# Four graph layers in one program: waits counted by tile, the symmetry proof's buffers kept into the next layer's prologue, and small loads moved to another queue

## The chip, the cores and the metric

The kernel runs on one core of one Trainium2 chip. A core has a matrix engine (PE, its weight loads listed apart as PEld), a vector engine (DVE), a scalar engine (ACT), GpSimd (POOL) and SyncE (SP), which here only issues transfers. Each takes its own list of instructions in order and waits for the others by semaphores. Transfers between the chip's memory and the on-chip memory are carried by 16 DMA engines, whichever engine issued them. The metric is the device time in microseconds (us); lower is better.

## The reference

Four layers of a graph network on 4096 nodes with 128 features share one dense adjacency matrix of 4096 x 4096 numbers, all 0 or 1, symmetric, with ones on the diagonal. Each layer's result is added to its input and normalised by rows.

```
x = layernorm(x + L0(x, adj))   # hyperbolic: sigmoid attention over distances, adj * sigmoid(logits) times local log maps
x = layernorm(x + L1(x, adj))   # 4 heads: softmax of q k / sqrt(32) where adj is not 0; then a gate with x @ Ws
x = layernorm(x + L2(x, adj))   # relu( D^-1/2 (adj + I) D^-1/2 x W )
x = layernorm(x + L3(x, adj))   # leaky_relu(s_i + r_j) where adj > 0, softmax by rows, times x @ W.T + b
```

The kernel may not assume that the matrix is symmetric and holds only 0 and 1. It runs a fast form that needs both, checks them on the way, and at the very end starts the general form (class `Net`) if a check failed. In the runs here the fast form (class `Fast`) does all the work.

## The kernel before

**Tiling.** The matrix is cut into 8 x 8 blocks of 512 x 512 (`NS` = 8, `S` = 512), each held as 128 partitions x 4 x 512. The program writes two copies of the blocks into the chip's memory: `adjb` in bf16 (0.5 MB a block) and `adjf` in float32 (1 MB a block).

**Layer 0** (L315 to L612). A prologue computes the nodes' hyperbolic features `HT` and `HA`. `pair_loop` (L1716) then goes over the 36 block pairs with I <= J in an order written out by hand (`SHARED_ORDER`, inside `manual_schedule`, where each engine gets its instructions in the order of the source). Meanwhile GpSimd's queue writes `adjb` (`narrow`, L1919). After the loop an epilogue (L514 to L612) brings the sums into `X` and normalises them, in groups of four row tiles: products of H and X (L540), squares (L544), scalings (L535), and at the end `X` normalised by ScalarE (L235).

**The proof of symmetry** (`mirror`, L1671 to L1709) is written into the source right after the pair loop. For each pair of blocks it loads `low` (block I, J; L1690) and `up` (block J, I; L1693), three buffers each, and PE forms `low` minus the transposed `up` with scaled identities (`sized`, L1684), twelve 128-row pieces in one psum bank `pm` (two buffers), each piece with its own power of two. DVE then takes the largest absolute value (L1709). There are 28 pairs and 8 diagonal blocks. This part and the epilogue are not ordered by hand: a scheduler orders each engine's instructions, by their place in the source (their priority) and by what it takes to be ready.

**Layer 1** (`layer1`, L2164). Its prologue (L2200 to L2255) transposes `X` into `XT` (L166, 32 times on PE), makes q and k for 8 column chunks (`pqk`, L2215), splits each into two float32r parts (`cut`, L2217 and L2218, seven buffers) and stores them to memory (`qk`, L2224, 16 stores of 0.5 MB). `stack` (L2192) reads them back on GpSimd's queue in another layout, as `KS` and `QS`. Then come V (`VA`, L2230 and L2231), R (in `Y`, L2240 and L2241), and a bound on the logits (`pb`, `good`). `attention_unshifted` (L1948) is again ordered by hand: for 8 column blocks I and 32 row tiles jb it does scores (`ps`, L2007), exponentials (`e`, L2014, ACT), the mask (L2016, DVE), and, two steps behind, the sums (`pv`, L2033, PE). At every fourth step SP loads the next `at` block from `adjb` (L1966) and copies one block to `adjf` (L1969); ACT's queue loads rows of the matrix (`nat`, L1983), for degrees and for the check that all entries are 0 or 1. `ending(I)` (L2042 to L2116) turns sums into `X` and the scaled node rows `Y`.

**Layers 2 and 3** (`layers23`, L2259). A ring of 8 float32 blocks (64 KB of each partition) is filled by SP from `adjf` (`load`, L2337). Layer 2 splits `Y` into two float32r parts (`halve`, L2359 to L2363: the node parts `Y0` and `Y1`) and multiplies them with 64 ring blocks (`convolve`, L2382; the first products, L2374, go by `identr`, a copy of the identity). DVE looks at each block once more (`look`, L2346). Eight blocks more start layer 3 (`attend_first`, L2400), whose other 56 follow in `attend_factored` (L1535 to L1580).

**Pools and waits.** Buffers come from pools that open and close like a stack. When a pool lands on bytes of pools already closed, all its tiles wait for every user of those pools. A tile is a buffer of such a pool.

Of the kernel before, what the change touches and what calls it, by code (L numbers as in the profile page):

```python
# [9 lines left out]
F32 = mybir.dt.float32  # L10
# [51 lines left out]
class Net:  # L62
# [30 lines left out]

    def copies(self):
        self.adjT = self.dram.tile([self.NS, self.NS, P, 4, S], F32, tag="adjT", name="adjT")

    def pools(self, ctx, adj, big, t, o):

        self.on_scalar = 4
        if adj:  # L100
            self.adjp = ctx.enter_context(self.tc.tile_pool(name="adjp", bufs=adj))
        if big:
            self.ps_big = ctx.enter_context(self.tc.tile_pool(name="ps_big", bufs=big, space=PSUM))
        self.ps_t = ctx.enter_context(self.tc.tile_pool(name="ps_t", bufs=t, space=PSUM))
        self.ps_o = ctx.enter_context(self.tc.tile_pool(name="ps_o", bufs=o, space=PSUM))
# [26 lines left out]
    def load_row(self, vec, name, pool=None):  # L132

        t = (pool or self.const).tile([P, vec.shape[0]], F32, tag=name, name=name)
        self.nc.sync.dma_start(out=t, in_=vec.partition_broadcast(P))
        return t
# [7 lines left out]
    def load_mat(self, mat, name, pool=None):  # L144
        t = (pool or self.const).tile(list(mat.shape), F32, tag=name, name=name)
        self.nc.sync.dma_start(out=t, in_=mat)
        return t
# [163 lines left out]
    def layer0(self, x, weight, bias, att_w, att_b):  # L311
# [4 lines left out]
        with ExitStack() as ctx:  # L316
            self.on_scalar = 4
            keep = ctx.enter_context(tc.tile_pool(name="keep0", bufs=1))
            self.cols = ctx.enter_context(tc.tile_pool(name="cols0", bufs=1))
            adp = ctx.enter_context(tc.tile_pool(name="ad0", bufs=2))  # L320
            pre_pools = ctx.enter_context(ExitStack())
            pre = pre_pools.enter_context(tc.tile_pool(name="pre0", bufs=2))
            self.ps_t = pre_pools.enter_context(tc.tile_pool(name="ps_t", bufs=6, space=PSUM))
            one = pre_pools.enter_context(tc.tile_pool(name="one0", bufs=1))
            self.wide = pre_pools.enter_context(tc.tile_pool(name="wide", bufs=1))
            ps_c = pre_pools.enter_context(tc.tile_pool(name="ps_c", bufs=1, space=PSUM))
# [187 lines left out]
            late = ctx.enter_context(tc.tile_pool(name="late0", bufs=1))  # L514
            rot = ctx.enter_context(tc.tile_pool(name="rot0", bufs=6))
# [92 lines left out]
    def pair_loop(self, HT, HA, dr, rows, adp, early, rows4):  # L608
# [7 lines left out]
        with ExitStack() as ctx:  # L616
            atp = ctx.enter_context(tc.tile_pool(name="at0", bufs=2))
            wtp = ctx.enter_context(tc.tile_pool(name="sg0", bufs=6))
            wk = ctx.enter_context(tc.tile_pool(name="wk0", bufs=2))
            ps_t = ctx.enter_context(tc.tile_pool(name="ps_t0", bufs=2, space=PSUM))  # L620
            ps_z = ctx.enter_context(tc.tile_pool(name="ps_z0", bufs=2, space=PSUM))
            ps_i = ctx.enter_context(tc.tile_pool(name="ps_i0", bufs=1, space=PSUM))
            ps_j = ctx.enter_context(tc.tile_pool(name="ps_j0", bufs=1, space=PSUM))
# [224 lines left out]
    def layer1(self, Wq, bq, Wk, bk, Wv, bv, Ws, bs, Wb, R):  # L848
# [6 lines left out]
        with ExitStack() as ctx:  # L855
            self.on_scalar = 4
            keep = ctx.enter_context(tc.tile_pool(name="keep1", bufs=1))
# [27 lines left out]
            with ExitStack() as pctx:  # L885
                pre = pctx.enter_context(tc.tile_pool(name="pre1", bufs=1))
                rot = pctx.enter_context(tc.tile_pool(name="rot1", bufs=2))
                self.ps_t = pctx.enter_context(tc.tile_pool(name="ps_t", bufs=8, space=PSUM))
# [59 lines left out]
    def attention_unshifted(self, VA, KS, QS, at0, stack, R, wb):  # L948
# [4 lines left out]
        with ExitStack() as ctx:  # L953
            rot = ctx.enter_context(tc.tile_pool(name="rotf", bufs=1))
            natp = ctx.enter_context(tc.tile_pool(name="natf", bufs=2))
            atp = ctx.enter_context(tc.tile_pool(name="atf", bufs=1))
            ep = ctx.enter_context(tc.tile_pool(name="ef", bufs=3))
            ps_s = ctx.enter_context(tc.tile_pool(name="ps_s", bufs=3, space=PSUM))
            ps_v = ctx.enter_context(tc.tile_pool(name="ps_v", bufs=1, space=PSUM))
# [198 lines left out]
    def attention_shifted(self, V, qk, R, wb, spare):  # L1158
# [4 lines left out]
        with ExitStack() as ctx:  # L1163
            self.pools(ctx, 1, 2, 3, 1)
            self.wide = ctx.enter_context(tc.tile_pool(name="wide", bufs=2))
            keep = ctx.enter_context(tc.tile_pool(name="keeps", bufs=1))
            self.cols = ctx.enter_context(tc.tile_pool(name="cols1", bufs=1))
# [12 lines left out]
            work = ctx.enter_context(tc.tile_pool(name="work1", bufs=1))  # L1180
# [98 lines left out]
    def layers23(self, w2, weight, bias, a_s, a_r, out, Y):  # L1279
# [6 lines left out]
        with ExitStack() as ctx:  # L1286
            RING = 8
            ring = ctx.enter_context(tc.tile_pool(name="ring", bufs=1)).tile([P, RING, 4, S], F32, tag="ring", name="ring")
            keep = ctx.enter_context(tc.tile_pool(name="keep3", bufs=1))
# [10 lines left out]
            pre = pctx.enter_context(tc.tile_pool(name="pre3", bufs=1))  # L1300
            rot = pctx.enter_context(tc.tile_pool(name="rot2", bufs=2))
            wp = pctx.enter_context(tc.tile_pool(name="w2", bufs=4))
            ps_b = pctx.enter_context(tc.tile_pool(name="ps_b", bufs=2, space=PSUM))
            ps_t = pctx.enter_context(tc.tile_pool(name="ps_t", bufs=2, space=PSUM))
# [1282 lines left out]
```

## Time and profile before

| what | us |
|---|---|
| median of 3 runs (lowest, highest) | 2021.89 (2018.53, 2024.26) |
| the profiled execution, its own time | 2022.37 |
| its span, first to last instruction | 2020.6 |

| stage | about, us from the span's start |
|---|---|
| layer 0: prologue | 0 to 75 |
| layer 0: pair loop | 75 to 643 |
| layer 0: epilogue, beside the proof of symmetry | 643 to 717 (proof to 742) |
| layer 1: prologue | 742 to 786 |
| layer 1: attention | 786 to 1600 |
| layer 2 and the start of layer 3 | 1601 to 1801 |
| layer 3 | 1801 to 2020 |

A profile page gives busy times of each engine, then the span in 40 slices. A row of a group or of the timeline names line, engine, operation and "output<-inputs", sizes, and in brackets how long the engine idled before it and what ended that. PE's busy time is modelled and counts pipelined products. The page's slices:

```profile
PE   4789999999998677999999999999999798899997
...
DVE  6579999898898846789998999999999888888986
...
DMA  3488999898934978996767676768656699978882
```

Each digit is the busy share of a fiftieth of a millisecond (50.5 us) in tenths. PE is nearly full but for the first slices, for slices 13 to 15 (657 to 808 us), where layer 0 ends and layer 1 begins, and for slice 31 (1566 to 1616), between attention and layer 2.

### The profile page before, as it was taken

The page shows a single profiled execution, that of the slowest core. Times are in us where ns is not written, and L with a number is a line of the kernel's source. Part 1 is how long each engine was busy: PE and PEld are TensorE (multiplying, and loading weights), DVE is VectorE, ACT ScalarE, POOL GpSimd, SP SyncE. Part 2 cuts the span into 40 slices and gives each one's busy share as a digit, 9 for nine tenths or more (in the row PEclk, how much of TensorE's full clock was granted, in tenths as well). Part 3 has the DMA queues.
Part 4 walks back from the last instruction along what each step waited for, and adds up shares of the span by engine and source line. Part 5 has one row for each costly group of instructions (what it writes and reads, how often), then busy time and mean ns, then how long its engine had stood idle before and what let it go on. Part 6 is the DMA issues. An engine that isn't in the chain of part 4 may idle for free.

```text
span 2020.6 us, 23440 instructions
## 1 busy us (share of the span) xinstructions
PE 1861.8 (92%) x8406; PEld 997.6 (49%) x8420; DVE 1738.0 (86%) x2741; ACT 1319.2 (65%) x1665; POOL 171.7 (8%) x269
## 2 busy tenths in 40 slices
PE   4789999999998677999999999999999798899997
PEld 4257776667667455333333333333333476644443
DVE  6579999898898846789998999999999888888986
ACT  5589999999997733777878787777877422210000
POOL 2212111121100311200000000000000000000000
PEclk8569999899998997999999999999999899999999
DMA  3488999898934978996767676768656699978882
GB/s 102 49 141 142 156 151 169 144 177 147 156 111 168 373 263 284 259 267 217 236 215 236 211 230 208 239 215 240 211 209 240 238 422 420 421 281 321 295 278 84
DMA packets 167247, 450.86 MB, mean 223 GB/s; under 512 B 13708, under 2 KB 56876, under 8 KB 142544
## 3 DMA queue, kind: packets, MB, share of 16 engines
q1 hardware_dynamic: 112128, 330.94, 45.3%
q0 software_dynamic: 45632, 50.69, 19.8%
q10 hardware_dynamic: 9360, 67.64, 10.4%
q8 instruction: 68, 1.11, 0.2%
q14 instruction: 59, 0.48, 0.1%
HBM read 472.20 MB, written 111.23 MB: 289 GB/s over the span
## 4 chain that ended last, share of the span: by engine, by line
PE 44%; DVE 25%; ACT 15%; DMA 11%; issue 5%; SPq 0%; ACTq 0%; POOL 0%; DVEq 0%; POOLq 0%
PE pv L2033 11%; PE pa L1576 10%; DVE e L2016 9%; PE ps L2007 6%; ACT e L2014 4%; DMA ring<-adjf 4%; PE pz L1782 4%; DMA up<-adjb 3%; PE pi L1866 2%; DVE nat L1998 2%; PE pj L1881 2%; ACT w L1799 2%; ACT s L1822 2%; PE pz L1785 2%; ACT y L1818 1%
## 5 line engine op out<-in xcount | busy, mean ns | idle before, releaser
L2016 DVE SCALAR_TENSOR_TENSOR e<-at,e 128x2048 f32<-128x2048 bf16 x256 | 582.7, 2286 | 78.4 <-ACT e L2014 77.8
L2014 ACT ACTIVATE e<-ps 128x1024 f32<-128x1024 f32 x512 | 493.1, 1024 | 150.0 <-PE ps L2007 122.0
L2033 PE MATMUL pv<-e,VA 128*64 128x512 f32 x2048 | 497.5, 607 | 6.4 <-DVE e L2016 6.1
L2007 PE MATMUL ps<-QS,KS 128*128 128x512 f32 x1024 | 314.4, 425 | 11.1 <-ACT e L2014 10.4
L2007 PEld LDWEIGHTS ps<-QS,KS 128*128 128x128 f32 x1024 | 170.5, 188 | 238.5 <-ACT e L2014 180.2
L2033 PEld LDWEIGHTS pv<-e,VA 128*64 128x64 f32 x2048 | 124.8, 136 | 250.2 <-issue 214.1
L1576 PE MATMUL pa<-w,Y 128*128 128x512 f32 x448 | 195.3, 594 | 0.0
L1782 PE MATMUL pz<-HT 128*128 128x512 f32 x288 | 173.5, 687 | 10.2 <-DVE w L1854 9.1
L1573 DVE SCALAR_TENSOR_TENSOR w<-rho,col,ring 128x512 f32<-128x512 f32 x224 | 162.8, 747 | 22.3 <-PE pa L1576 9.7
L1866 PE MATMUL pi<-HA,w 128*128 128x129 f32 x1152 | 157.5, 286 | 7.3 <-ACT s L1822 5.3
L1866 PEld LDWEIGHTS pi<-HA,w 128*128 128x128 f32 x1152 | 144.0, 199 | 19.1 <-issue 9.3
L2382 PE MATMUL pa<-ring,Y 128*128 128x512 f32 x512 | 133.1, 411 | 11.9 <-DVE ring L2357 10.0
L1576 PEld LDWEIGHTS pa<-w,Y 128*128 128x128 f32 x448 | 83.7, 190 | 106.1 <-issue 79.9
L1989 ACT ACTIVATE nat<-nat 128x2048 f32<-128x2048 f32 x64 | 122.5, 1915 | 4.1 <-DMA nat<-in_adj_dram 4.1
L1791 DVE TENSOR_SCALAR t<-pz 128x512 f32<-128x512 f32 x144 | 93.7, 684 | 30.3 <-PE pz L1785 30.3
L1881 PE MATMUL pj<-HA,w 128*128 128x129 f32 x896 | 117.5, 288 | 2.1 <-DVE X L1895 1.8
L2382 PEld LDWEIGHTS pa<-ring,Y 128*128 128x128 f32 x512 | 95.9, 192 | 42.3 <-DVE ring L2357 12.8
L1881 PEld LDWEIGHTS pj<-HA,w 128*128 128x128 f32 x896 | 109.9, 200 | 9.9 <-issue 7.2
L1854 DVE TENSOR_TENSOR w<-w,ptz 128x512 f32<-128x512 f32 x112 | 73.7, 681 | 23.5 <-PE ptz L1849 23.3
L1799 ACT ACTIVATE w<-di,dr 128x512 f32<-128x512 f32 x144 | 90.6, 708 | 1.9 <-DMA di<-rows 1.9
L2346 DVE SCALAR_TENSOR_TENSOR odd<-ring 128x1024 bf16<-128x1024 f32 x64 | 78.1, 1220 | 12.8 <-DMA ring<-adjf 12.3
L1830 DVE SCALAR_TENSOR_TENSOR t<-t,s 128x2048 f32<-128x2048 f32 x36 | 82.3, 2285 | 6.7 <-ACT s L1822 6.7
(410 smaller groups left out, 2338.5 us busy)
## 6 DMA issues: line engine op xcount, KB each, us to landing
ring<-adjf SPq DMA_DIRECT2D x128, 1024.0 KB, 12.9
nat<-in_adj_dram ACTq DMA_DIRECT2D x64, 1024.0 KB, 6.0
adjf<-in_adj_dram SPq DMA_DIRECT2D x64, 1024.0 KB, 7.4
ad<-in_adj_dram SPq DMA_DIRECT2D x36, 1024.0 KB, 9.2
adjb<-in_adj_dram POOLq DMA_DIRECT2D x64, 512.0 KB, 11.5
at<-adjb SPq DMA_DIRECT2D x63, 512.0 KB, 3.5
low<-adjb SPq DMA_DIRECT2D x36, 512.0 KB, 5.5
up<-adjb SPq DMA_DIRECT2D x28, 512.0 KB, 6.7
```

Of the source, the lines that this page charges most:

```text
L1573: nc.vector.scalar_tensor_tensor(w, rho[:, I * S : (I + 1) * S], col[:, 0, j : j + 1], at[:, jb, :], op0=ALU.max, op1=ALU.mult)
L1576: nc.tensor.matmul(pa, lhsT=F[:, j, :], rhs=w, start=False, stop=(j == NT - 1), skip_group_check=True)
L1782: nc.tensor.matmul(pz, lhsT=HT[:, j * P : (j + 1) * P], rhs=HT[:, I * S : (I + 1) * S], start=True, stop=False)
L1799: nc.scalar.activation(w[:, jb, :], st[p]["d"][k], AF.Sigmoid, bias=dr[:, 4 * J + jb : 4 * J + jb + 1])
L1866: nc.tensor.matmul(row[I, "po"][ib // 2][:, ib % 2, :], lhsT=st[p]["w0"][:, jb, ib * P : (ib + 1) * P], rhs=HA[:, 4 * J + jb, :], start=False,
L1881: nc.tensor.matmul(pj[:, a, :], lhsT=st[p]["w1"][:, ib, jb * P : (jb + 1) * P], rhs=HA[:, 4 * I + ib, :], start=(ib == 0), stop=(ib == 3),)
L1989: nc.scalar.activation(nat, nat, AF.Identity, accum_out=self.deg2[:, k, i : i + 1])
L2007: nc.tensor.matmul(p[:, h, :], lhsT=KS[:, h2 + h, jb * P : (jb + 1) * P], rhs=QS[I % 2][:, h2 + h, :], start=True, stop=True,)
L2014: nc.scalar.activation(e[:, h2 : h2 + 2, :], p, AF.Exp)
L2016: nc.vector.scalar_tensor_tensor(e, at[:, jb % 4, :].unsqueeze(1).to_broadcast([P, NH, S]), 0.0, e, op0=ALU.not_equal, op1=ALU.mult,)
L2033: nc.tensor.matmul(st["po"][h // 2][g : g + 64, :], lhsT=VA[:, o : o + 64], rhs=e[:, h, :], start=(jb == 0), stop=(jb == NT - 1), skip_gro ...
L2382: nc.tensor.matmul(st["pa"], lhsT=halves[k][:, j, :], rhs=at[:, jb, :], start=(I > 0 and j == k == 0), stop=(j == NT - 1 and k == 1), skip ...
```

## The change

Four things. (1) The pools of the fast form are opened with `reuse_waits="tile"`: a tile that lands on bytes of closed pools waits only for the users of earlier tiles on its own bytes (in psum, its own bank). (2) The proof's three pools no longer close with layer 0. They are opened on the other side of the on-chip memory (`side="right"`), kept in `self.proof`, and close with layer 1's prologue; the prologue is given a priority ahead of the proof's (`high_priority`, from `self.rank`, which is the proof's place). To make room, the prologue has six psum banks for eight and five `cut` buffers for seven. (3) The node parts `Y0` and `Y1` get a pool of their own directly behind the ring. (4) The small loads of layers 2 and 3 (`w2`, `br3`, `wn3` and the three columns `ac`) go by GpSimd's queue, not SP's.

```diff
+    waits = "pool"
+
+    def pool(self, **kw):
+        return self.tc.tile_pool(reuse_waits=self.waits, **kw)
+
...
-    def load_row(self, vec, name, pool=None):
+    def load_row(self, vec, name, pool=None, queue=None):
...
-        self.nc.sync.dma_start(out=t, in_=vec.partition_broadcast(P))
+        (queue or self.nc.sync).dma_start(out=t, in_=vec.partition_broadcast(P))
...
-    def load_mat(self, mat, name, pool=None):
+    def load_mat(self, mat, name, pool=None, queue=None):
...
-            keep = ctx.enter_context(tc.tile_pool(name="keep0", bufs=1))
+            keep = ctx.enter_context(self.pool(name="keep0", bufs=1))
...
 class Fast(Net):
 
     MARKS = 160
+    waits = "tile"
...
-        keep = ctx.enter_context(tc.tile_pool(name="mir", bufs=1))
-        rot = ctx.enter_context(tc.tile_pool(name="mirt", bufs=3))
-        ps = ctx.enter_context(tc.tile_pool(name="mirp", bufs=2, space=PSUM))
+        self.proof, self.rank = ExitStack(), tc.cur_priority
+        keep = self.proof.enter_context(self.pool(name="mir", bufs=1, side="right"))
+        rot = self.proof.enter_context(self.pool(name="mirt", bufs=3, side="right"))
+        ps = self.proof.enter_context(self.pool(name="mirp", bufs=2, space=PSUM, side="right"))
...
             with ExitStack() as pctx:
-                pre = pctx.enter_context(tc.tile_pool(name="pre1", bufs=1))
-                rot = pctx.enter_context(tc.tile_pool(name="rot1", bufs=2))
-                self.ps_t = pctx.enter_context(tc.tile_pool(name="ps_t", bufs=8, space=PSUM))
+                pctx.enter_context(self.proof)
+                pctx.enter_context(tc.high_priority(tc.cur_priority - self.rank + 1))
+                pre = pctx.enter_context(self.pool(name="pre1", bufs=1))
+                rot = pctx.enter_context(self.pool(name="rot1", bufs=2))
+                self.ps_t = pctx.enter_context(self.pool(name="ps_t", bufs=6, space=PSUM))
...
-                        cut = rot.tile([P, 2, S], F32R, tag="cut", name="cut", bufs=7)
+                        cut = rot.tile([P, 2, S], F32R, tag="cut", name="cut", bufs=5)
...
+            halved = ctx.enter_context(self.pool(name="halved", bufs=1))
+            halves = [halved.tile([P, NT, D], F32R, tag=f"Y{k}", name=f"Y{k}") for k in range(2)]
...
-            halves = [pre.tile([P, NT, D], F32R, tag=f"Y{k}", name=f"Y{k}") for k in range(2)]
...
-            w = self.load_mat(w2, "w2")
-            br = self.load_row(bias, "br3", keep)
-            wn = self.load_mat(weight, "wn3", pre)
+            w = self.load_mat(w2, "w2", queue=nc.gpsimd)
+            br = self.load_row(bias, "br3", keep, nc.gpsimd)
+            wn = self.load_mat(weight, "wn3", pre, nc.gpsimd)
...
-                nc.sync.dma_start(out=ac[:, k : k + 1], in_=v.unsqueeze(1))
+                nc.gpsimd.dma_start(out=ac[:, k : k + 1], in_=v.unsqueeze(1))
```

All other pools of the layers change from `tc.tile_pool(...)` to `self.pool(...)` in the same way as `keep0`; the pools of constants, of `X` and of the memory copies do not. No arithmetic is added or left out.

## The prediction

> **What bounds the kernel now.** I read the whole-page view first: TensorE (PE) is busy 92% of 2020.6 us, VectorE (DVE) 86%. An average hides where a change of waits can pay, so I went on to the slices of the page, which dip at two places, and asked the waits, the chain of waits and the timeline there. The first place is the end of layer 0 and the prologue of layer 1. The chain of waits (start, length, what):
>
> ```profile
> 728.21 4.99 DMA low<-adjb
> ...
> 742.50 3.69 PE pt L166 x32
> ...
> 773.48 14.82 DMA qk<-cut
> ...
> 795.91 3.61 PE pv L2033 x8
> ...
> 800.85 1.87 PE pv L2033 x8
> ```
>
> and what was waited for between 640 and 800 us (total, times, longest):
>
> ```profile
> POOL VA L2204 <- PE pm L1704: 54.3, 1, 54.3
> ...
> ACT XT L181 <- PE pt L166: 27.6, 1, 27.6
> ...
> ACT L2014 <- DMA qk<-cut: 16.4, 1, 16.4
> ```
>
> The proof of symmetry (L1690 to L1709) runs from 643 to 741.7 and only then layer 1's first transposition starts, at 742.50. Its input was ready long before; ScalarE's last normalising of X:
>
> ```profile
> 715.65 1.65 ACT L235 ACTIVATE X<-X,ms,rs 128x128 f32<-128x128 f32 x4 [0.44 <-DVE ms L229]
> ```
>
> So X waits 25.2 us (717.3 to 742.5) for the proof. The table of windows gives the DMA share (second number from the end) and GB/s (last):
>
> ```profile
> 716.00:720.00 4.00, 2.36 (x21) 1.25 (x20) 0.21 (x1) 1.29 (x4) 0.00 (x0) 1.00 1.01 379
> 724.00:728.00 4.00, 3.37 (x41) 2.43 (x40) 0.69 (x1) 0.00 (x0) 0.00 (x0) 1.00 0.68 212
> 744.00:748.00 4.00, 4.00 (x26) 2.98 (x24) 1.84 (x4) 2.80 (x6) 1.48 (x1) 1.00 0.11 43
> 764.00:768.00 4.00, 1.95 (x8) 1.65 (x8) 1.95 (x3) 1.38 (x2) 1.64 (x3) 0.72 1.14 382
> ```
>
> Proof and prologue are each limited by transfers, one after the other, and between them the DMA engines are half empty. The second place is the step from attention to layer 2 (timeline of the SP queue, of PE, and windows):
>
> ```profile
> 1587.58 1.97 SPq L2337 DMA_DIRECT2D ring<-adjf  x4
> 1600.41 0.33 SPq L135 DMA_DIRECT2D br<-in_L_gnn_b_dram  x1
> ...
> 1602.68 22.43 SPq L2337 DMA_DIRECT2D ring<-adjf  x13
> ```
>
> ```profile
> 1601.38 2.20 PE L2374 MATMUL pa<-identr,Y 128*128 128x128 f32 x8 [12.55 <-ACT Y L2362]
> ```
>
> ```profile
> 1590.00:1600.00 10.00, 0.00 (x0) 0.00 (x0) 8.66 (x45) 0.92 (x5) 0.00 (x0) 0.59 0.91 383
> 1600.00:1610.00 10.00, 8.61 (x34) 7.17 (x34) 7.71 (x18) 5.64 (x9) 0.00 (x0) 0.73 0.68 252
> 1610.00:1620.00 10.00, 10.00 (x49) 8.29 (x48) 9.05 (x22) 0.00 (x0) 0.00 (x0) 1.00 1.01 421
> ```
>
> PE idles 12.55 us, the fifth ring block is issued 13 us after the fourth, and from 1610 to 1780 the DMA share is 1.01: layer 2 is bound by its 1 MB blocks. Elsewhere there is nothing for waits to win: attention has PE busy 99% in the windows from 900 to 1400, layer 3 100% from 1800 to 1900. A shift made at either place therefore reaches the end.
>
> **What the Trainium skill says.** "PSUM — Partial Sum Buffer", section "Engine vs sequencer instructions": ScalarE, VectorE and GpSimd queues are strict FIFO, and matmuls start and complete in program order. The trace agrees (742.50 directly follows the proof's last matmul), so PE's order decides what can lie beside what. "DMA: Bandwidth & Descriptors", section "Issuing engines are not separate DMA queues": transfers from SP, ACT and GpSimd share the same 16 engines, and another queue saves issue time alone. The trace agrees: one queue or two, the share tops out near 1.0 to 1.15. No page bears on the rule by which a pool waits; I read that from the programs' instruction lists.
>
> **The change, part by part** (line numbers of before).
>
> *Proof beside the prologue.* The lists show what the scheduler made of it: PE does 361 of the proof's 678 matmuls, then mixes 125 more with the 32 transpositions, then pqk, V and R products with 50 between; 142 come after R, 90 of them in one lump just before the third step's scores and the first pv. SP issues 27 of 28 block pairs, all 16 qk stores, and then the last pair and the 8 diagonal blocks. DVE's first masking of e stands behind the proof's last reduction. So the prologue can start when X is ready, but the first pv still waits for the whole proof. That makes it a sum over the DMA engines.
> Start: the first three pairs no longer wait for the pair loop's last matmul, but for a DVE step near 627, so they are there when PE is free at 643. From 643 the engines must move: 58 blocks x 0.524 MB = 30.4 MB at 372 GB/s (mean of the windows 644 to 724) = 81.7 us; at0, 16 stores of 0.524 and 16 loads of 0.262 MB = 13.1 MB at 381 (windows 760 to 784) = 34.4; one at, one adjf and one nat block, 2.6 MB at 370 = 7.1. Together 123.2, to 766.2 if they never rest. X does not hold this up: PE reaches the 361st matmul (18 pairs) near 691 and waits for the first X to about 697 (701.4 in before, less about 4 for the part below), but three pairs are in flight meanwhile. After the stores there are rests: the last pair and the diagonal come through three buffers, and a low block takes 5.5 us from issue to landing. Three rests of 3 us: 9 us (bounds 0 and 24). The proof ends at 775; its reduction 0.7 and the first e (2.29) bring the first pv to 778 and the second to 781, since e of later steps follows at 2.2. Before, the second pv was at 800.85. Gain 20 (29 to 5). The ps and e work that lay between (two table loads, three rounds) now hides under the proof's last blocks.
> Fewer buffers: cut 7 to 5, psum 8 to 6. In before the 12th cut already waits for stores; with five outstanding the engines still have 2.6 MB queued, so nothing to 2 us, in the range.
>
> *Waits by tile at the end of the pair loop.* DVE idles 4.4 us before 642.9 and ACT 11.1; the 24 scalings (2.5 us, L1684) and 28 of 32 squares (L544) move into that. Worth about 4 us on X, but X is not what comes last (see the sum); only the start of the loads counts, included above. At the pair loop's start the first pz waits for the copy of rows ending near 75.0 instead of the e2 step at 75.5: 0 to 0.7, I take 0.3.
>
> *Attention to layer 2.* The ring lies on KS. Its first load waited for the last pv (1587.49); by the list it now waits for the last ps (1580.87), and the six small loads that stood in SP's queue behind the fourth block (their tiles waited for the ending, 1600.4) are on GpSimd, so eight blocks go at once. Before, 0.36 + 3.83 + 2.52 MB moved by 1610; at 420 GB/s that is 16.0 us, as if saturated from 1594.0. After: 1580.9 plus the 1.5 us that before took from issue to flow (1587.6 to about 1589.1) = 1582.4. Gain 11.6. It holds while the engines never starve: a slot comes free when DVE has looked and PE has multiplied. Node parts (halve) now wait on VA's and QS's last users, 1587.5, not on the ending; identr is ahead of the ending on DVE, and PE starts near 1589.6 instead of 1601.4. DVE then carries the ending (10.4 us busy) between looks: eight looks by about 1614, one per 3 us against 2.6 for a block, with eight blocks of slack; enough. Over the stage DVE has 155.5 + 10.4 us of work in 180, PE 164 in 179. I take 11 (7 to 12).
> The GpSimd loads: w2 falls between two squares at 10.6 to 19.1, where POOL idles; wn waits for the last pv, then 64 KB, about 2.2 us by the skill's page on DMA ("Anatomy of one DMA — SWDGE (gpsimd) path": 2.0 us plus bytes/436 GB/s, an estimate; the 4 KB el loads here take 3.2). That is 1591; the products that need it come after three groups of 2.08 us, about 1596. Hidden; without that cover 1 to 3 us, but nobody queues behind it on POOL.
>
> *Sum:* 20 + 11 + 0.3 = 31. The profiled execution took 2022.37 (span 2020.6 and 1.8 around it), the median of the runs 2021.89: the same to 0.03%. 2022.4 - 31 = 1991.
>
> **Rivals.** (1) *The tail of the proof eats the gain.* The last pair and diagonal, behind the stores, meet adjf and nat, and each three-buffer turn takes as long as in the diagonal phase of before or longer (8 blocks in 14.3 us there). The proof ends near 790, the second pv at 796: gain 5 + 11 = 16, 2006. For: 142 matmuls in PE order before the first pv. Against: 3 us per block is twice what before needed.
> (2) *Layer 2 is not DMA bound once moved.* DVE with ending, parts and looks starves the slots, gain 3 there: 1999. For: DVE waits for ring in all only 12.3 us. Against: share 1.01 for 170 us.
> (3) *Slower.* One mechanism: SP's order. The at blocks of attention stand between proof blocks, which wait for PE, whose scores and pv stand behind the proof; a stalled store thus holds proof, attention and nat together. It decides from a first pv later than about 813 (795.9 + 11.3 won elsewhere + 6), 35 us past my 778; with the first pv at 826, 30 us later than before, the time is 2022.4 + 30 - 11 = 2041. Against: the same bytes would have to move at three quarters of the measured rates.
> (4) *It doesn't do what it says:* excluded by the lists for order; whether waits fall is rivals 1 and 2.
>
> **How the numbers follow.** Forecast 0.62 (1983 to 2000), rival 1 0.20, rival 2 0.10, rival 3 0.08. The range takes 1981 (proof's rests at nought: 29 + 12) to 2007 (rival 1), leaving out rival 3 and some of each edge. About 0.3%, 6 us, is what a measurement here can tell from no change. Faster: all of forecast and rival 2, most of rival 1, 0.89; within 0.3%: the edge of rival 1 and of 3, 0.05; slower 0.06.
>
> **What would show it.** First pqk near 714 (746.0 before) and no wait of POOL's VA memset for pm; DMA share near 1 from 645 to 760 without the dip at 744; first pv between 772 and 784; ring loads eight in a row from the last ps on; PE's gap before L2374 under 2 us. Wrong if the first pv comes after 790, if ring loads stop for more than 5 us before 1620's counterpart, or if attention itself (first pv to end of the last, 791.6 us) changes by more than 5 us.

## The result, and the profile after

| | before | after |
|---|---|---|
| median of 8 runs each, us | 2024.21 (2016.38 to 2028.32) | 2007.49 (1999.29 to 2012.74) |
| the profiled execution | 2022.37, span 2020.6 | 1999.29, span 1997.4 |

Ratio 0.9916, 95% interval 0.9893 to 0.9939: about 17 us, where 31 were forecast. A second series (six runs against eleven) gave 1998.89 against 2022.33, ratio 0.9884 (0.9855 to 0.9914). The two agree within their intervals, so the gain is 12 to 29 us as timed, and some 20 us if both are taken together. The traced execution was the fastest of the first eight, so I read stages from it beside two more traces of the same kernel; the one of the second series (1999.15 us) lies at that series' median.

The page's slices of the changed kernel (each digit is the busy share, in tenths, of 49.9 us, a twentieth of a millisecond; slices are counted from 0):

```profile
PE   4669999999998687999999999999999898899997
...
DMA  3468989899945896996767676768666899968881
```

PE still dips in slices 13 to 15 (649 to 799 us); in slice 31 it has 8 tenths for 7. Waits between 640 and 800 us (total, times, longest):

```profile
PEld pt L171 <- ACT X L240: 12.1, 15, 7.6
...
ACT e L2021 <- PE pm L1711: 10.6, 1, 10.6
```

The two long waits of before (POOL's memset of VA, and XT, both for the proof) have gone. Two new ones name the price: PE waits for X at a transposition, and the exponentials wait for the proof's products. The chain of waits:

```profile
692.39 0.86 PE pt L171 x2
...
713.75 0.88 PE pqk L2224 x2
...
768.74 7.24 DMA low<-adjb
...
782.13 2.29 DVE e L2023
784.55 1.94 PE pv L2040 x8
...
787.62 1.87 PE pv L2040 x8
```

The prologue's first product for q and k (`pqk`) starts at 713.75 instead of 746.0, yet the first pv only at 784.55 instead of 795.85, and the load just ahead on the chain is one of the proof's. The table of windows (the third number from the end is the clock, then DMA share and GB/s) shows where the transfers rest:

```profile
680.00:690.00 10.00, 3.86 (x40) 2.49 (x40) 8.02 (x32) 4.57 (x7) 3.65 (x1) 0.87 0.96 368
690.00:697.00 7.00, 4.61 (x25) 3.16 (x26) 6.35 (x36) 3.31 (x10) 0.00 (x0) 0.50 0.02 8
...
776.00:784.00 8.00, 7.13 (x50) 4.98 (x51) 2.48 (x2) 2.48 (x3) 0.00 (x0) 0.79 0.07 27
```

PE's timeline and SP's tell why:

```profile
684.75 0.38 PE L1706 MATMUL pm<-low,sized 128*128 128x512 bf16 x1
692.39 0.86 PE L171 MATMUL pt<-ident,X 128*128 128x128 f32 x2 [7.27 <-ACT X L240]
```

```profile
685.13 0.38 SPq L1700 DMA_DIRECT2D up<-adjb  x1
696.34 0.32 SPq L1697 DMA_DIRECT2D low<-adjb  x1
```

PE came to the first transposition at 685 and stood there for 7.27 us until X was normalised. The proof's three pairs of buffers were held for products that PE had still to do, SP issued no load from 685.13 to 696.34, and the engines emptied. In the kernel before, the empty stretch lay between the proof and the prologue:

```profile
740.00:749.00 9.00, 8.04 (x57) 5.99 (x57) 4.37 (x7) 3.63 (x7) 3.65 (x1) 1.00 0.18 60
```

Summed in steps of 1 us, the idle DMA time is 18.4 us from 643 to the first pv before, and 20.6 us from 640 to the first pv after. The rests have moved; they are not fewer.

At the second place, the step to layer 2, PE's timeline:

```profile
1571.47 0.33 PE L2384 MATMUL pa<-identr,Y 128*128 128x128 f32 x1
1572.79 1.00 PE L2384 MATMUL pa<-identr,Y 128*128 128x128 f32 x7 [0.99 <-DVE Y L2373]
...
1581.18 0.35 PE L2321 MATMUL pu<-ac,wn 128*128 128x2 f32 x2 [1.88 <-DMA ac<-in_L_gnn_a_r_dram]
```

The gap of 12.55 us has become 0.99. The ring's first load is issued at 1563.79, with the last scores (1563.3), and eight follow in a row, the eighth at 1567.32.

### The profile page after: what moved, and what is told of

It is laid out like the page before. It is cut to its first block, busy times and chain, and to the rows that moved or that the text cites. A ratio compares the mean times of both kernels' runs of the same rounds, so it can differ in the third digit from the quotient of the medians.

```text
span 1997.4 us, 23428 instructions
## 1 busy us (share of the span) xinstructions
PE 1831.7 (92%) x8405; PEld 988.5 (49%) x8420; DVE 1736.9 (87%) x2741; ACT 1318.3 (66%) x1665; POOL 172.1 (9%) x275
## 3 DMA queue, kind: packets, MB, share of 16 engines
q1 hardware_dynamic: 111264, 330.74, 46.1%
## 4 chain that ended last, share of the span: by engine, by line
PE 41%; DVE 27%; ACT 18%; DMA 9%; issue 4%; SPq 0%; POOL 0%; ACTq 0%; DVEq 0%; POOLq 0%
PE pv L2040 10%; DVE e L2023 10%; PE pa L1581 10%; PE ps L2014 6%; ACT e L2021 4%; DMA ring<-adjf 3%; ACT w L1806 3%; DVE nat L2005 3%; PE pi L1873 2%; PE pj L1888 2%; ACT s L1829 2%; ACT y L1825 2%; PE pz L1789 2%; ACT y L1821 2%; ACT nat L1996 1%
## 5 line engine op out<-in xcount | busy, mean ns | idle before, releaser
L1581 PE MATMUL pa<-w,Y 128*128 128x512 f32 x448 | 195.3, 594 | 0.0
L1789 PE MATMUL pz<-HT 128*128 128x512 f32 x288 | 157.1, 628 | 22.1 <-DVE t L1798 12.2
L1581 PEld LDWEIGHTS pa<-w,Y 128*128 128x128 f32 x448 | 83.7, 190 | 106.1 <-issue 80.5
```

The costliest lines, as they stand in the source:

```text
L1581: nc.tensor.matmul(pa, lhsT=F[:, j, :], rhs=w, start=False, stop=(j == NT - 1), skip_group_check=True)
L1789: nc.tensor.matmul(pz, lhsT=HT[:, j * P : (j + 1) * P], rhs=HT[:, I * S : (I + 1) * S], start=True, stop=False)
```

## The experiments

All sixteen are read by four stages: the pair loop (first `pz` to the proof's first product), the middle (from there to the end of the last pv), the step to layer 3's first product (L1581; L1576 before), and layer 3. These stages do not add up to the span: the prologue's 75 us come first. One column more, "from last pz", runs from the start of the loop's last `pz` to the end of the last pv; the reason follows the table. All from the traces, us; ratios are to the kernel before, timed in the same series, with 95% intervals.

| kernel | ratio | loop | middle | from last pz | to layer 3 | layer 3 |
|---|---|---|---|---|---|---|
| before | 1 | 571.3 | 940.7 | 981.9 | 213.7 | 219.4 |
| e11: before again | | 572.6 | 939.2 | 981.0 | 213.8 | 219.4 |
| after | 0.9916 (0.9893 to 0.9939) | 561.5 | 933.6 | 971.0 | 206.6 | 220.5 |
| e12: after again | | 563.9 | 933.9 | 971.9 | 207.0 | 220.2 |
| e13: after, timed again | 0.9884 (0.9855 to 0.9914) | 561.3 | 934.6 | 971.8 | 205.8 | 220.3 |
| e1: waits by tile alone | 0.9908 (0.9881 to 0.9935) | 563.9 | 934.5 | 973.4 | 210.8 | 218.1 |
| e5: those of layer 0 alone | 0.9940 (0.9918 to 0.9961) | 575.5 | 936.0 | 973.1 | 212.0 | 218.1 |
| e6: those after layer 0 alone | 0.9977 (0.9964 to 0.9991) | 567.8 | 941.9 | 983.2 | 211.7 | 219.4 |
| e2: waits, proof beside prologue | 0.9907 (0.9880 to 0.9935) | 566.7 | 933.8 | 969.4 | 208.8 | 218.2 |
| e3: waits, layer 2 part | 0.9893 (0.9869 to 0.9917) | 566.1 | 937.3 | 976.2 | 207.9 | 220.2 |
| e14: e3 again | 0.9910 (0.9879 to 0.9942) | 562.9 | 937.9 | 976.8 | 205.4 | 220.3 |
| e4: after, without the proof | 0.9831 (0.9801 to 0.9861) | | | 957.8 | 205.3 | 219.8 |
| e7: transpositions held | 0.9904 (0.9874 to 0.9935) | 565.8 | 937.2 | 974.5 | 206.2 | 220.2 |
| e8: e7, six buffers, columns | 0.9897 (0.9868 to 0.9927) | 566.8 | 938.0 | 973.6 | 207.0 | 218.2 |
| e9: held until the tenth | 0.9865 (0.9830 to 0.9900) | 562.2 | 930.0 | 967.3 | 204.8 | 218.2 |
| e15: e9 again | 0.9870 (0.9835 to 0.9905) | 563.7 | 932.1 | 967.7 | 204.2 | 218.2 |
| e10: held until the ninth | 0.9875 (0.9848 to 0.9901) | 563.0 | 932.3 | 969.7 | 205.1 | 218.1 |
| e16: proof first, six buffers | 0.9873 (0.9839 to 0.9906) | 568.0 | 929.8 | 967.0 | 206.6 | 218.2 |

The pair loop itself, from its first to its last `pz`, takes 530.0 and 530.8 us in the two traces of before, 526.5 in e6 (with the old waits there), 538.3 in e5, and 524.0 to 531.2 in the others. Kernels with the old and the new waits overlap, so this part is not shown to belong to the change; "from last pz" leaves it out, and agrees within 1 us wherever one kernel was traced twice or more. From the last `pz` to the end of the span the changed kernel is 16 to 17 us shorter than before (17 and 23 by its ratios), e1 13 (19), e5 12 (12) and e6 1 (5). What the ratios have beyond that lies in the loop or in the spread between executions, and stays open.

### The parts, one at a time

**Waits by tile alone (e1).** Against the changed kernel: the proof closes with layer 0 again, and node parts and small loads are where they were.

```diff
-        self.proof, self.rank = ExitStack(), tc.cur_priority
+        self.proof = ctx
...
-                pctx.enter_context(self.proof)
-                pctx.enter_context(tc.high_priority(tc.cur_priority - self.rank + 1))
...
-                self.ps_t = pctx.enter_context(self.pool(name="ps_t", bufs=6, space=PSUM))
+                self.ps_t = pctx.enter_context(self.pool(name="ps_t", bufs=8, space=PSUM))
...
-            w = self.load_mat(w2, "w2", queue=nc.gpsimd)
+            w = self.load_mat(w2, "w2")
```

> Theory A: the gain is a sum of three separate places, and the rule for waits carries little of it by itself. With the proof closed before the prologue as before, it starts about 3 us earlier because its first loads no longer wait for the pair loop's last product; the ring's first loads start with the last scores, but the small loads in SP's queue still stop the fifth block until the ending. Gain 3 to 6 us, ratio to the kernel before 0.997 to 0.9985. Theory B: the waits by tile are what helped, and the moves of the proof and of the small loads little: gain 12 us or more, ratio 0.994 or lower.

2004.82 against 2025.87 us, ratio 0.9908: theory A falls, B stands. As far as these runs can tell, the one rule carries as much as the whole change (0.9916 and 0.9884). The chain of waits of e1:

```profile
733.78 3.50 PE pt L171 x32
737.28 0.88 PE pqk L2222 x2
...
784.13 3.61 PE pv L2040 x8
```

With the proof wholly ahead of the prologue, the first pv comes at 784.13, where the changed kernel with its overlap has 784.55. The proof's first product stands at 639.6 for 646.8. Of these 7.1 us, 4.8 are the pair loop, which varies anyway; 2.3 come with the proof's first loads, issued at 633.44 (642.89 before). From the loop's last `pz`, e1 gains 8.5 us up to the last pv: the 2.3, 2.9 between the first `pqk` and the first pv, 1.6 in the attention, and the rest in the proof and just behind it.

**Proof beside the prologue (e2), layer 2 part (e3).** e2 leaves out parts 3 and 4 of the change, e3 leaves out part 2 (the first six changed lines of the diff above, and seven `cut` buffers).

> Waits by tile and the proof beside the prologue, with node parts and small loads as before. Theory A: second pv about 13 us earlier than in the kernel before (787 to 790), layer 2 as in the run with waits alone; ratio 0.993 to 0.9945, 11 to 14 us. Theory B (the clock or the crowding of transfers takes back what the overlap gives): second pv earlier by no more than 6 us over several executions, ratio about 0.997.

> Waits by tile, node parts behind the ring and small loads on GpSimd's queue, with the proof before the prologue as in the kernel before. Theory A: from the last pv to layer 3's first product 7 us less than before (about 206.7 for 213.7), plus the 3 us at the proof's start: ratio 0.995 (10 us). Theory B (this part is worth all that the whole change gained): ratio 0.992, 16 us. A third reading (layer 2 gives nothing that lasts): ratio 0.998.

e2: 2005.80 us, ratio 0.9907; its second pv, at 792.7, is 8 us early and not the 13 of A. e3: 2003.00, ratio 0.9893, below both of its theories. Neither can be told from e1 or from the whole by its time. In the stages, the layer 2 part shortens the step to layer 3 by some 3 us more (210.8 in e1, 208.8 in e2; 207.9 and 205.4 in e3 and e14); A's 206.7 lies between the last two. The proof beside the prologue is worth 4 to 5 us from the last `pz` on: 969.4 in e2 for 973.4 in e1, and 971.0 to 971.9 in the whole for 976.2 and 976.8 in e3 and e14.

**Which waits (e5, e6).** e1, with one line at the start of layer 1 that sets the rule for all later pools: "tile" in layer 0 and "pool" after it (e5), or the reverse (e6).

```diff
             self.on_scalar = 4
+            self.waits = "pool"
             keep = ctx.enter_context(self.pool(name="keep1", bufs=1))
```

> Waits by tile in layer 0 and the proof alone; every later pool waits as before, and the proof, node parts and small loads stand as before. Theory A (the pair loop itself gains: in all runs with waits by tile PE had its full clock from 76 us on, in the kernel before only from 132): clock 1.00 in the windows 80 to 90 again, first product of the proof near 640 for 646.8, first pv near 788, ratio 0.995 to 0.996. Theory B (that clock was chance in the one execution of the kernel before that was profiled): only the proof's first loads gain, ratio 0.998 to 0.999.

> Waits as before in layer 0 and the proof, by tile from layer 1 on, all else as before. Theory A: clock 0.5 in the windows 80 to 130 as in the kernel before, first product of the proof near 647; then 3 us less in the prologue of layer 1 (46.8 from the first pqk to the first pv for 49.8), 2 in the first steps of the attention, 3 from the last pv to layer 3: ratio 0.996. Theory B (the clock was chance): first product of the proof near 641, ratio 0.993.

2016.61 us (0.9940) and 2020.70 (0.9977, above both of its theories). The ratios' gains, 6.0 and 2.3 thousandths, make 8.3, near e1's 9.2. The larger share is layer 0's: from the last `pz` to the last pv e5 takes 973.1, as e1 does, and e6 983.2, as the kernel before. 4.1 of the 8.8 us that e5 gains there lie ahead of the proof's first product; the others are spread behind it. The step to layer 3 is near 212 in both. e5's first product of the proof came at 650.6, not near 640 as A had it, because its traced pair loop was the longest of all (538.3).

**Without the proof (e4).** `pairs = []` in `mirror`.

> Leaves out the comparison of the matrix with its transpose: no loads, products or reductions of the proof. It bounds what the proof still costs in the changed kernel. Theory A (the proof's transfers and its products, which stand ahead of the first pv in PE's order, set the start of the attention): first XT transposition about 692 as now, prologue then as long as before the change (742.5 to the first pv at 795.9, 53 us), so first pv near 748 for 784.6, and the time 35 us below that of the changed kernel, ratio to the kernel before about 0.975. Theory B (the prologue itself, above all storing and reading back q and k, sets the start): first pv after 770, ratio 0.985 or more.

1988.26 us, ratio 0.9831; first pv at 768.6, from a first pqk at 715.2. That is near theory B, just outside both of its marks, and far from A: the prologue by itself takes 53.4 us, and for 30 of them (725 to 755) storing and reading back q and k fill the DMA engines (share 1.13 to 1.15). In these traces the proof thus still costs 16 us on the first pv (784.6 to 768.6), and the medians differ by 11 to 17 us (0.9831 for 0.9884 and 0.9916), so a better order of it could hardly win more.

### Why the overlap gave so little

**Filling the hole (e7, e8).** The transposition uses a copy of the identity that DVE makes only after the proof's eighth reduction, so that PE has products and SP has free buffers while X is not ready. e8 also lets the diagonal blocks use both kinds of buffers, and loads the three columns `ac` at the program's start (`self.const`).

```diff
+                ident, later = self.ident, pre.tile([P, P], F32, tag="later", name="later")
+                nc.vector.scalar_tensor_tensor(
+                    later, ident, self.odd[:, 7 : 8], ident, op0=ALU.mult, op1=ALU.add
+                )
+                self.ident = later
                 self.transposed(X, XT)
+                self.ident = ident
...
-                low = up = rot.tile([P, 4, S], BF16, tag="low", name="low")
+                side = "up" if I == J and I % 2 else "low"
+                low = up = rot.tile([P, 4, S], BF16, tag=side, name=side)
```

> The changed kernel, with the transpositions of X made to wait for the proof's eighth reduction (24 pairs), so that PE has work and SP free buffers while X is not ready. Theory A (in the changed kernel PE stands at the first transposition from 685 to 692 with no free buffer behind it, DMA share 0.26 from 690 to 700, and this is what the overlap lost): no such hole, first pqk near 707 for 713.6, first pv near 777 for 784.6, ratio to the kernel before 0.988. Theory B (what the hole lost comes back as a wait in the proof's tail or in the stores): first pv after 782, ratio 0.991 to 0.992.

> As the run with the transpositions held, and the diagonal blocks take the low and the up buffers in turn (six for three), and the three columns of layer 2 are loaded at the start of the program. Theory A (the tail from 760 to 782 is short of buffers, DMA share 0.66 from 770 to 780; PE's waits of 3.3 us for the columns are on layer 2's path): first pv near 773, and 204 us from the last pv to layer 3 for 206.7; ratio 0.984 to 0.986. Theory B (the tail is held by PE's order, layer 2 by its blocks): first pv as in the run with the transpositions held, within 2 us, layer 2 the same; ratio equal to that run's within 0.002.

Both miss A: first pv at 791.9 and 788.8, ratios 0.9904 and 0.9897, near theory B. A window of e7, then PE and DVE in its hole:

```profile
710.00:720.00 10.00, 6.22 (x31) 6.25 (x32) 5.30 (x18) 4.61 (x12) 0.00 (x0) 0.51 0.16 55
```

```profile
713.78 6.57 PE L171 MATMUL pt<-later,X 128*128 128x128 f32 x32 [6.46 <-DVE later L2218]
```

```profile
712.48 0.16 DVE L234 SCALAR_TENSOR_TENSOR ms<-mv,rs 128x4 f32<-128x4 f32 x1
712.56 0.68 DVE L1716 TENSOR_REDUCE odd<-pm 128x1 f32<-128x512 f32 x1
713.28 0.35 DVE L2218 SCALAR_TENSOR_TENSOR later<-ident,odd 128x128 f32<-128x128 f32 x1
```

The hole at 690 was filled and opened again 20 us later (share 0.16). PE reached the held transpositions at 707.3 and stood 6.46 us, now for `later` itself: DVE took the eighth reduction only at 712.56, behind its last step on X. The last pair and the diagonal blocks stood in SP's queue behind the sixteen stores. The six buffers did fill the tail (share 1.03 from 770 to 780, 0.66 in the changed kernel), and it moved the first pv by 3 us. The early columns left the step to layer 3 as it was (207.0; 206.2 in e7), so PE's waits for them were not what it lasts for. They show elsewhere: layer 3 takes 218.2 for 220.2. It is 219.8 to 220.5 in every trace in which GpSimd's queue loads the columns beside layer 2, 219.4 in before and e6, and 218.1 to 218.2 in all others. From the first of layer 3's products to the last it takes 205.7 us in each; the 2 us lie in the closing waits behind the last output transfer. Why was not tried.

**Holding longer (e9, e10, e15), and not overlapping at all (e16).** e9 and e10 are e8 with `self.odd[:, 9 : 10]` and `[:, 8 : 9]`; e16 is e3 with the six buffers and the early columns.

> As the run with six buffers, but the transpositions wait for the proof's tenth reduction (28 pairs and 2 diagonal blocks), so that all of the proof's loads stand ahead of the stores of q and k in SP's queue. Theory A (the overlap loses because the proof's loads stop twice: while PE or SP waits for X with no free buffer, and behind the stores): no window of 10 us with a DMA share under 0.8 from 650 to 760, last proof reduction before 760, first pv near 777, 923 us from the proof's first product to the end of the last pv (930.5 in the changed kernel, 935 with waits alone), ratio 0.985 to 0.987. Theory B (moving transfers about within the stage gives nothing, whatever the order): 932 to 938 us there, ratio 0.989 to 0.992.

> The same with the ninth reduction (27 pairs); four loads of diagonal blocks stay behind the stores. Theory A: X not delayed by the proof (first pqk near 716), one short tail; first pv 777 to 780, ratio 0.986 to 0.988. Theory B: as the run with the eighth, first pv near 789, ratio 0.990.

> The version held until the tenth reduction, timed beside the changed kernel. Theory A (the two stops of the proof's loads were what the overlap lost): 5 to 8 us faster than the changed kernel, ratio to the kernel before 0.986 to 0.988. Theory B (its earlier time was a good series of executions): within 3 us of the changed kernel.

> The proof before the prologue, with the other three parts of the change, six buffers for the diagonal blocks and the early columns; no overlap at all. Theory A (the proof's transfers, not the order, are the limit, and three buffers leave the engines idle in the diagonal part, DMA share 0.71 from 710 to 720): last reduction 3 us earlier than 733.6 to 737.0, 2 us off layer 2, ratio 0.988 to 0.989, between the run without the buffers and the held one. Theory B (the overlap gives nothing once loads do not stop): equal to the held one within 2 us.

> The changed kernel, timed beside the three that follow. Theory A (each kernel's time is what its stages show): ratio to the kernel before 0.990 to 0.9915. Theory B (it loses 3 us or more against the waits alone through the overlap): 0.992 or more.

> The proof before the prologue as in the kernel before, with waits by tile, node parts behind the ring and small loads on GpSimd's queue, timed beside the changed kernel. Theory A (laying the proof beside the prologue gave about 2 us): 1 to 3 us slower than the changed kernel, 0.991 to 0.992. Theory B (it cost time): faster than the changed kernel by 3 us or more, 0.9885 to 0.9895.

The first series gave e9 1993.93 us (0.9865) and e10 1995.93 (0.9875). In the second, all on one chip: after 1998.89, e14 2003.52, e15 1995.39, e16 1998.81, the kernel before 2022.33. By ratio e9 and e10 meet theory A. By the other signs they do not: in e9 and e15 the first pv came at 778.5 and 781.6, the last reduction of the proof ended at 772.1 and 775.0 and not before 760, e9's DMA share was 0.63 from 720 to 730, and the middle is 930 and 932, not 923; e10's first pv came at 781.0. e15 is 3.5 us faster than the changed kernel, between its theories; e16, at 0.9873, is faster than A and 3.4 us from the held version, where B had 2; the changed kernel's 0.9884 is below both theories, and e14, 4.6 us slower than it, is nearest A. (The 930.5 of e9's and e12's expectations, and e12's 564.5, count the changed kernel's first product of the proof 3 us late; the table's 933.6 and 561.5 are from the same trace.) Windows of e15 and of e16:

```profile
641.00:700.00 59.00, 42.59 (x421) 27.26 (x419) 51.65 (x259) 46.28 (x213) 20.09 (x25) 0.97 0.97 361
...
728.00:732.00 4.00, 4.00 (x16) 2.17 (x15) 1.85 (x4) 3.54 (x7) 0.00 (x0) 1.00 0.11 42
```

```profile
638.00:718.00 80.00, 56.92 (x569) 37.98 (x568) 65.69 (x355) 56.09 (x239) 15.64 (x24) 0.98 0.99 372
718.00:728.00 10.00, 9.41 (x114) 7.16 (x112) 2.07 (x3) 0.00 (x0) 0.00 (x0) 1.00 0.96 372
728.00:738.00 10.00, 9.60 (x74) 7.13 (x71) 4.97 (x8) 4.16 (x8) 3.66 (x1) 1.00 0.21 73
```

e16 keeps the engines full through the diagonal part (0.96 from 718 to 728; 0.76 from 727 to 740 in the kernel before), then has its gap between proof and prologue as the other kernels without overlap do, and its middle, 929.8, equals the held version's; so does the time from the last `pz` (967.0; 967.3 and 967.7). Six buffers and no overlap reach in these stages what the overlap reaches with the same buffers and its loads kept going. Without overlap, e16 is 9 us shorter there than e3 and e14, which lack the buffers: they did more than the overlap. e9 and e15 have the lowest medians of the versions that do all the work, 3.5 us under the changed kernel on the same chip, but the intervals overlap: that they, or e16, beat it is likely and not shown.

**Second traces (e11, e12).**

> The kernel before once more, for a second trace. If the half clock from 76 to 130 belongs to it: 0.5 again in the windows 80 to 130, 569 to 571 us from the pair loop's first product to the proof's first product, 941 from there to the end of the last pv, 213.8 from there to layer 3. If it was chance: full clock from 76 and about 565 in the first of these.

> The changed kernel once more, for a second trace. If the profiled execution was a lucky one in places (it was the fastest of eight): a span near 2005, with the pair loop's part 3 to 6 us longer than 564.5 and the other stages within 2 us of 930.5 and 206.7. If stages differ between executions as much as between kernels, these too will be off by 4 us or more.

Single executions took 2022.80 and 2002.12 us. In before and after, stages behind layer 0 repeat within 1.5 us; so do the loops of before, and those of after within 2.6. The pairs e3, e14 and e9, e15 differ by up to 2.5 in a stage.

## Why the prediction was wrong, by its own steps

**The sum over the DMA engines** was right in its bytes (46.1 MB foreseen; the trace of after has 47.2 MB from 640 to the first pv at 784.6) and wrong in its rests, the times in which the engines move nothing:

| term of the sum | forecast, us | measured, us |
|---|---|---|
| transfers | 123.2 | 124.0 |
| rest while PE waits for X | 0 | 7.9 (688 to 698) |
| rests behind the stores | 9 | 1.1 (763 to 776) |
| last transfer to first pv | 3 | 8.4 (776 to 784.6) |
| other rests | 0 | 3.1 |

The first failed step is "X does not hold this up". PE's wait itself was foreseen well (691 to 697; it was 685.1 to 692.4), but three pairs in flight were to cover it. They cover no more than the time that the engines take to move them, and free no buffer while PE stands: "three buffers" was counted for the tail and not for this wait. The second is the way from the last transfer to the first pv, "its reduction 0.7 and the first e (2.29)": it left out PE's products on the last blocks, which ended at 781.5. The "Three rests of 3 us" hardly came where they were placed. By luck their 9 us stood in for part of the others, and the sum began earlier than foreseen (PE's first product of the proof at 636.7 for 643, in an execution with a short pair loop); otherwise the miss would have been larger.

**The first pv** came at 784.55 (forecast 778; the line drawn was 772 to 784), the second at 787.62 (781): gain 13.2 for 20. None of that is shown to be the overlap's. e1 has the first pv at 784.13 without it, and counted from the last `pz` it comes after 183.3 us in e1 and 183.9 in e2, 185.2 and 186.9 in e3 and e14 and 185.2 to 185.7 in the whole (190.3 and 189.3 before). e13 beside e14 shows 4.6 us in the medians (not separable by their intervals), 3.3 in the middle and 5.0 from the last `pz`; these lie in the attention, see below. The step "Worth about 4 us on X, but X is not what comes last" was another error. In the kernel before everything waits for the proof, and e5, where only the waits of layer 0 and the proof are by tile and nothing overlaps, gains 8.8 us from the last `pz` on. The waits by tile had that gain alone; I gave all of it to the overlap. First pqk near 714 was right (713.6), as were the waits that would go; the share near 1 from 645 to 760 was not (0.02 from 690 to 697).

**Attention** was to stay as it was. From second pv to the end of the last it took 782.7 us for 786.7, and from the first pv 785.7 for 791.6, outside the 5 us that I had set as a test. In e2, e12 and e13 it is 785.5 to 786.2 from the first pv, in e7 787.1; with the proof first and any waits by tile 789.8 to 791.1; in e8 and the versions held until the ninth or tenth 789.6 to 791.0. The short form goes with a first pv that follows the proof's last product directly: after 3.1 us in the changed kernel, e2, e7, e12 and e13, and after 7 or more in all others. Why was not tried. It is also 4.3 of the 7 us that the held version's middle missed; the rest is the late count of the 930.5.

**Attention to layer 2**: gain 11 (7 to 12) forecast, 7.1 measured, 6.7 and 8.0 in the other two traces. The mechanism was right: ring loads start with the last scores, and PE's gap is 0.99 us. From the ring's first load to 45 us behind the last pv, 16.2 MB moved before and 20.1 after, at 420 GB/s a lead of 9.3 us. Of it 8.7 us arrive at the first product of `attend_first` (173.9 us behind the last pv before, 165.2 after), and 1.7 are lost from there to layer 3's first product (39.8 and 41.5); what holds that part back stays open. So the step that failed here is "A shift made at either place therefore reaches the end": three quarters of this one did. At `attend_first`, e1 has 169.9 and e2 169.1, e3 and e14 166.3 and 164.9: about half is due to the waits by tile, half to the parts and small loads. "Hidden" was wrong for the small loads in this trace: beside eight ring blocks `wn` took 5.1 us from issue to landing for the estimated 2.2, the columns 6.4 to 8.4, and PE waits 1.88 us for a column; but e8 shows that this step does not become shorter without the wait.

**The loop's start** came 0.37 us earlier (0.3 forecast). The loop with the proof's start was 7 to 11 us shorter than in the two traces of before, of which the sum took in about 4 by starting at 643. 3 to 5 us of it lie between the last `pz` and the proof's first product (41.2 and 41.8 before; 37.2 to 38.0 after), as the sum had it; the rest is the loop itself, not shown to be the change's.

**Sum**, in the traced executions: second pv 13.2, attention 4.0, step to layer 3 7.1, layer 3 -1.2, together 23 for 31, and the first series' median lies another 8 us above its traced execution. Where that spread arises stays open: no execution near that median was traced. Rival 1's 2006 is nearest the first median, but not its mechanism: the proof ended at 782, not 790. Rival 2 (3 us in layer 2) is excluded by 7; rival 3 by the first pv.

## What to carry to other kernels

Before crediting an overlap, ask how much of its gain a simpler part of the same change already takes: here releasing layer 0's end and the proof's first loads from a coarse wait won more than the overlap did, and twice the buffers in one short part won it again without reordering. In a sum over a shared resource the bytes are the easy part; find each place where a consumer in program order can stand still while it holds all the buffers, and count the resource as idle there from the moment that the last buffer fills. And trace a kernel more than once before a few microseconds of a stage are explained.

## What the runs showed of the hardware

PE's granted clock stayed at half for long in 5 of the 18 traced executions, although PE was busy throughout. In the second trace of the kernel before:

```profile
76.00:112.00 36.00, 36.00 (x41) 11.01 (x42) 12.86 (x15) 22.64 (x16) 8.84 (x14) 0.50 0.59 70
```

and in that of the changed kernel, which has the same products there:

```profile
76.00:96.00 20.00, 17.86 (x37) 5.63 (x36) 8.66 (x11) 13.97 (x11) 8.08 (x14) 0.99 0.99 117
```

It was 0.50 from 76 to 112 in both traces of before and in e6, e7 and e10, and 0.94 to 1.00 from 76 to 96 in the others. The products' length agrees: the median of the `pz` from `HT` between 76 and 96 was 1.06 to 1.22 us in the five, and 0.64 to 0.70 in the others. The Trainium skill ("TensorE: Matmul & The Clock Gate", section "Part 1: The HAM clock gate") has the clock released after about 3.4 us of sustained work; from 76 to 112 us it was not. The page's own caveat, of a clock seen stuck for over 50 us, is nearest, but it speaks of a quarter clock. The end of the loop does not show the difference: its last `pz` starts between 601.8 and 606.8 in the five, and between 598.9 and 613.5 in the others.
